# Cross-attention's mask and bias moved into the last row of the keys

## Chip, cores and metric

One core of a Trainium2 chip runs the whole program. The metric is device time in microseconds of that core, the median of several runs. TensorE is called PE below, VectorE DVE, ScalarE ACT, GpSimd POOL; the DMAs are issued by SyncE (SP).

## What is computed

Four blocks in a row: a memory-gated cross-attention (L0), a single-head cross-attention (L1), a six-layer transformer decoder (L2) and a last cross-attention with layer norm (L3). The batch is 8, a sequence has 256 rows of 128 features, the context 64 rows of 64 features. Nearly all of the time goes to the six layers of L2, and the change is in L2's cross-attention:

```python
def _mha(s, t, kv_w, q_w, o_w, o_b, mask):          # 16 heads of 64
    k, v = jnp.split(s @ kv_w, 2, axis=-1)
    q = t @ q_w
    k, v, q = (_heads(k), _heads(v), _heads(q))
    scores = jnp.einsum('bhqd,bhkd->bhqk', q, k) * D ** (-0.5)
    scores = jnp.where(mask[:, None] == 0, jnp.float32(-1000000000.0), scores)
    attn = jax.nn.softmax(scores, axis=-1)
    o = jnp.einsum('bhqk,bhkd->bhqd', attn, v)
    return o.transpose(0, 2, 1, 3).reshape(t.shape[0], t.shape[1], H * D) @ o_w + o_b

def step(t, p):                                      # scanned over 6 layers
    tn = _ln(t, norm_g, norm_b)
    t = _mha(tn, tn, skv, sq, sow, sob, tgt_mask) + t
    tn = _ln(t, norm_g, norm_b)
    t = _mha(src, tn, ckv, cq, cow, cob, src_mask) + t
    tn = _ln(t, pg, pb)
    t = t + (jax.nn.relu(tn @ w1 + b1) @ w2 + b2)
```

`_ln` subtracts the mean, divides by the root of variance plus 1e-5, then multiplies by a gain and adds a bias, one per feature.

## The kernel before

All activations stay in SBUF in f32: `t` holds 16 tiles of 128 rows by 128 features, two per batch entry. The program is not written as a loop. Functions enter steps into a plan with `at(tick, phase, fn)`; at the end the ticks are walked in order, and within a tick the steps in the order of their phase. Each compute engine keeps exactly that order (a manual dependency ties every instruction to the one before it on its engine), so a step with phase 3.7 stands in each engine's queue ahead of one with phase 6 of the same tick, whatever it waits for. DMAs on SP's queue come in program order.

In a layer, self-attention takes 4 ticks per batch entry, 32 in all, then cross-attention takes 2 ticks per entry, 16 in all. `T_ca` is the first tick of the cross-attention. The feed-forward of entry b starts 7 ticks after its cross-attention, and the next layer's self-attention begins inside the cross-attention's last ticks.

PSUM is one pool of four tiles of two banks (lines 35 to 50: `psum`, `two_banks`, with `one_bank`, `tp_tile` and `mm_tile` taking the first half of one). They are handed out in turn, so that a matmul group which asks for a tile waits until the reader of the tile handed out four requests before is done.

The cross-attention of one batch entry (`plan_ca`, with T = T_ca + 2b) works so:

- `ahead` (line 842) makes the normalised input: `moments` on DVE (phase 6 of tick T - 4; `bn_stats` and `bn_aggr`, lines 849 and 850), `scales` on POOL at phase 8.4 (lines 855 to 862: epsilon added, power of -0.5, mean times it, negated), `normal` on ACT (line 868), and `trans` on PE, evicted by ACT with the norm's gain as scale and the norm's bias as bias (lines 882 and 884). Self-attention uses `ahead` too, with `normal` on DVE (line 873), and so does the feed-forward.
- `plan_ca_weights` folds, once per layer, the key and query weights into `AT` and the value and output weights into `WVO` (lines 1083 to 1096). Its first step stands six ticks ahead of T_ca.
- `keys_both` (line 1107) makes the keys of two entries with 16 matmuls (line 1120) into two PSUM tiles, and ACT copies them to SBUF (line 1126). It stands at phase 3.7 of tick T - 2 of every even entry, so at T_ca - 2, + 2, + 6 and + 10.
- `plan_weights_64` (line 329) does one tile of 128 query rows per tick: `scores` (matmuls of line 356, then the mask's matmuls of line 363: bf16, a row of ones against the row of masks `nm2`, accumulated on top), `lower` (ACT copies the scores to SBUF in line 372, DVE takes the maxima per head from PSUM in line 374, POOL subtracts them in line 375), `exps` (ACT, line 381), `divide` (DVE sum and reciprocal, lines 385 and 386, POOL multiplies, line 387), `turn` (DVE transposes, line 395) and `sums` (PE, line 429; DVE adds the residual, line 1145). L0 uses the same function with `mask` None.

Around the change there are also self-attention's `exps` (DVE line 953, ACT line 958), `divide` (DVE line 966, POOL line 968), `turn` (DVE line 978), `values` (PE line 994), `out_proj` (PE line 1012, at phase 3.1) and `add_out` (DVE line 1019, at phase 8.2, which reads `out_proj`'s PSUM tile). The last two of batch entries 6 and 7 fall into the ticks T_ca - 2 and T_ca + 2.

Of the kernel before, what the change touches and what calls it, by code (L numbers as in the profile page):

```python
# [27 lines left out]
def tile_xattn_stack(ctx: ExitStack, tc: tile.TileContext, io, out: bass.AP):  # L28
# [125 lines left out]
    norm_g = column("L2_norm_g")  # L154
    norm_b = column("L2_norm_b")
    pre_g = load_const("L2_pre_gT", [D, NL])
    pre_b = load_const("L2_pre_bT", [D, NL])
# [106 lines left out]

    nm2 = const.tile([P, B, M], BF16, tag="nm2", name="nm2")
    nc.vector.memset(nm2, 0.0)
    ones0 = const.tile([P, 32], BF16, tag="ones0", name="ones0")
    nc.vector.memset(ones0, 0.0)
    nc.vector.memset(ones0[0:1], 1.0)

# [57 lines left out]

    def plan_weights_64(tick, qt, qT, keys, values, mask, take):

# [4 lines left out]
        def scores():  # L335
            sc = two_banks("sc").rearrange("p (q x) -> p q x", q=4)
            if mask is None:
                for i in range(4):
# [14 lines left out]
            for q in range(4):  # L353
                qb = 4 * qt + q
                for a in range(4):
                    nc.tensor.matmul(  # L356
                        sc[32 * a : 32 * a + 32, q, :],
                        lhsT=qT()[:, qb * 32 : (qb + 1) * 32],
                        rhs=keys()[:, a].rearrange("p h k -> p (h k)"),
                        start=True, stop=False,  # L360
                    )
                for a in range(4):
                    nc.tensor.matmul(
                        sc[32 * a : 32 * a + 32, q, :], lhsT=ones0, rhs=mask,
                        start=False, stop=True,
                    )
            tl["sc"] = sc.rearrange("p q x -> p (q x)")

        def lower():
            sc = tl.pop("sc")  # L370
            e = big("e", shape=(P, 16, M))
            nc.scalar.copy(e.rearrange("p h k -> p (h k)"), sc)  # L372
            m = sm([P, 16], "m16")
            nc.vector.tensor_reduce(m, sc.rearrange("p (h k) -> p h k", k=M), AX.X, ALU.max)  # L374
            nc.gpsimd.tensor_tensor(  # L375
                e, e, m.unsqueeze(2).to_broadcast([P, 16, M]), ALU.subtract
            )
            tl["e"] = e
# [12 lines left out]
        def turn():  # L391
            e = tl.pop("e").rearrange("p (q h) (k x) -> p (h k) q x", q=4, x=32)
            eT = big("k" if mask is None else "o", shape=(P, 8, 4, 32))
            for i in range(2):
# [41 lines left out]
        at(tick, 2, lower)  # L436
        if mask is None:
            at(tick + 1, 2.05, exps)
# [197 lines left out]
    def mask_keys():  # L636
        mi = big("q", dtype=I32)
        mi = mi[0:1, : B * M].rearrange("p (b m) -> p b m", b=B)
        nc.sync.dma_start(out=mi, in_=io["mask_Bx1xS2_if1"].rearrange("b o m -> o b m"))
        nc.vector.tensor_scalar(nm2[0:1], mi, 0.0, -BIG, ALU.is_equal, ALU.mult)  # L640

# [41 lines left out]
    def plan_l0(b, T):  # L683
# [88 lines left out]
        for qt in range(QT):  # L772
            plan_weights_64(
                T + qt, qt, lambda: st["q"], lambda: st["k"], lambda: st["VW"], None,
                lambda ps, qt=qt: add(qt, ps),
            )
# [66 lines left out]
    def ahead(b, stats_at, normal_at, tT_at, g, bias, st, on_scalar=True):  # L843

        def moments():
            st["mv"] = sm([P, QT, 2], "mv")
            for j in range(QT):
                six = sm([P, 6], "six")
                nc.vector.bn_stats(six, tt(b)[:, j, :])
                nc.vector.bn_aggr(st["mv"][:, j, :], six)  # L850

        def scales():
            mv = st["mv"]
            ve = sm([P, QT], "ve")
# [191 lines left out]
    def plan_ca_weights(l, T):  # L1046
# [55 lines left out]
        at(T + 1, 8.05, regrouped)  # L1102
        at(T + 2, 3.6, folded("AT", 0, lambda c: st[1][:, :, c, :], HD ** -0.5))
        at(T + 3, 3.6, folded("WVO", 1, lambda c: W["ca", l][2][:, c, :]))

    keys_of = {}

    def plan_ca(l, b, T):
# [3 lines left out]
        def keys_both():  # L1112

            res = [big("q", shape=(D, 4, 4, M)) for _ in range(2)]
            for g in range(2):
# [9 lines left out]
                for i in range(2):  # L1125
                    nc.scalar.copy(
                        res[i][:, :, 2 * g : 2 * g + 2, :].rearrange("p a r k -> p r a k"),
                        ps[:, :, :, i * M : (i + 1) * M],
                    )
            keys_of[b], keys_of[b + 1] = res  # L1130
# [6 lines left out]

        ahead(b, (T - 4, 6), (T - 3, 2.95), (T - 2, 2.9), norm_g, norm_b, st)
        if b % 2 == 0:
# [7 lines left out]
        for qt in range(QT):  # L1147
            plan_weights_64(
                T + qt, qt, lambda: st["tT"], lambda: keys_of[b], lambda: st["VW"],
                nm2[:, b].unsqueeze(1).to_broadcast([P, 4, M]), lambda ps, qt=qt: add(qt, ps),  # L1150
            )
# [229 lines left out]
```

## Time and profile before

| | |
|---|---|
| Time, three runs | median 2428.22 us (2428.0 to 2430.0) |
| The profiled execution's own time | 2429.18 us |
| Its span, first to last instruction | 2427.5 us |
| Mean granted PE clock | 0.984 of full speed |
| PE busy | 2334.8 us (96%) |
| DVE busy | 1833.6 us (76%) |
| ACT busy | 1708.2 us (70%) |
| POOL busy | 1418.0 us (58%) |
| Mask matmuls, line 363 | 1536, 113.6 us busy, 276 ns each, four at a time |
| Score matmuls, line 356 | 3072 records, 221.8 us busy |
| Key copies on ACT, line 1126 | 96, 49.3 us |
| Maxima on DVE, line 374 | 112, 136.7 us |
| Epsilon on POOL, line 855 | 144, 31.7 us |
| Negation on POOL, line 862 | 96, 21.8 us |

An f32 matmul shows as two records. Busy time is the union of an engine's intervals, and a matmul's end is modelled, so a busy PE is not PE at its peak. "Idle before" in a row is the time in which the engine did nothing just ahead of that instruction, with the instruction that ended it behind the arrow. Times of day are microseconds from the start of the span. A layer is about 373 us: line 356 first runs at 395.1 us in the first layer and at 768.0 us in the second. In the second layer, which is used below, T_ca - 2 begins at 754.2 us, T_ca at 768.0, T_ca + 2 at 777.6, T_ca + 3 at 786.9, T_ca + 10 at 833.0.

### The profile page before, as it was taken

The numbers are of one execution on the slowest core, as the hardware profiler recorded it, in microseconds if no ns is written. First come the engines' busy times: TensorE is split into PE (matmuls) and PEld (weight loads), VectorE is DVE, ScalarE is ACT, GpSimd is POOL, SyncE is SP. The second block draws the span as 40 slices with busy tenths as digits, with TensorE's granted clock in tenths as the row PEclk, the third lists the DMA queues.
The fourth block names the chain that finished last, engine by engine and source line by source line (L and its number), as shares of the span: only waits on it lengthen the run. The fifth ranks groups of instructions, "written<-read, shape, count | busy, mean of one in ns | idle before, by whom it ended". The sixth has DMA issues, their size and how long they took to land.

```text
span 2427.5 us, 100277 instructions
## 1 busy us (share of the span) xinstructions
PE 2334.8 (96%) x42564; PEld 1726.5 (71%) x42564; DVE 1833.6 (76%) x5997; ACT 1708.2 (70%) x4514; POOL 1418.0 (58%) x2471
## 2 busy tenths in 40 slices
PE   7889999999999999999999999999999999999997
PEld 4557777677777777777777777777777677777775
DVE  5678887667887767888667888667888667888675
ACT  4567777667777667777667778567778657777653
POOL 2445556755556754556765555765555765455774
PEclk9989999999999999999999999999999999999998
DMA  6000022001022001012000012000013000001000
GB/s 178 2 11 12 20 73 65 2 3 30 21 68 69 2 3 30 20 60 68 12 3 28 22 53 74 12 2 18 25 44 84 21 1 18 25 27 40 2 4 16
DMA packets 102833, 76.88 MB, mean 32 GB/s; under 512 B 8113, under 2 KB 96881, under 8 KB 102386
## 3 DMA queue, kind: packets, MB, share of 16 engines
q1 hardware_dynamic: 101794, 70.16, 9.9%
q8 instruction: 334, 5.47, 0.9%
q14 instruction: 113, 0.93, 0.1%
q10 hardware_dynamic: 592, 0.33, 0.1%
HBM read 62.07 MB, written 8.39 MB: 29 GB/s over the span
## 4 chain that ended last, share of the span: by engine, by line
PE 79%; DVE 8%; ACT 7%; POOL 5%; issue 1%; DMA 0%; ACTq 0%; POOLq 0%; DVEq 0%
PE sc L939 14%; PE mm L902 14%; PE mm L994 14%; PE mm L1012 7%; PE mm L921 7%; PE mm L429 5%; PE sc L356 4%; PE mm L1178 3%; PE mm L1161 3%; DVE m L374 2%; PE mm L1120 2%; PE tp L882 1%; ACT e L958 1%; ACT e L372 1%; PE mm L318 1%
## 5 line engine op out<-in xcount | busy, mean ns | idle before, releaser
L968 POOL TENSOR_SCALAR e<-e,rs 128x256 f32<-128x256 f32 x1536 | 703.0, 478 | 682.4 <-DVE rs L966 673.2
L958 ACT ACTIVATE e<-e,mn 128x256 f32<-128x256 f32 x1536 | 758.2, 495 | 141.6 <-DVE mn L953 137.4
L953 DVE CUSTOM_DVE_ANT_0 e<-sc,nm 128x256 f32<-128x256 f32 x1536 | 542.3, 419 | 102.3 <-PE sc L939 102.1
L978 DVE STREAM_TRANSPOSE eTc<-e 128x512 f32<-128x512 f32 x768 | 517.3, 695 | 62.1 <-POOL e L968 60.9
L939 PE MATMUL sc<-k,q 64*32 64x256 f32 x12288 | 381.0, 383 | 1.1 <-ACT v L301 0.6
L994 PE MATMUL mm<-eTc,v 32*64 32x256 f32 x12288 | 363.6, 378 | 5.7 <-ACT AT L1095 3.3
L375 POOL TENSOR_TENSOR e<-e,m 128x1024 f32<-128x1024 f32 x112 | 213.0, 1902 | 225.3 <-DVE m L374 225.3
L994 PEld LDWEIGHTS mm<-eTc,v 32*64 32x64 f32 x12288 | 277.4, 131 | 88.5 <-issue 22.3
L374 DVE TENSOR_REDUCE m<-sc 128x16 f32<-128x1024 f32 x112 | 136.7, 1220 | 242.7 <-ACT e L372 242.7
L939 PEld LDWEIGHTS sc<-k,q 64*32 64x32 f32 x12288 | 222.0, 107 | 124.0 <-issue 51.4
L958 ACT ACTIVATION_READ_ACCUMULATOR e<-e,mn 128x1 f32 x1536 | 287.1, 187 | 0.0
L356 PE MATMUL sc<-q,tT 128*32 128x256 f32 x3072 | 221.8, 388 | 2.3 <-DVE t L1145 2.3
L429 PE MATMUL mm<-v,o 128*128 128x128 f32 x1536 | 199.8, 285 | 0.2 <-ACT v L324 0.2
L429 PEld LDWEIGHTS mm<-v,o 128*128 128x128 f32 x1536 | 186.3, 198 | 15.9 <-issue 8.1
L902 PE MATMUL mm<-tT,w_sk 128*128 128x256 f32 x768 | 189.3, 389 | 0.0
L1012 PEld LDWEIGHTS mm<-w_sow,o 128*128 128x128 f32 x1536 | 175.1, 192 | 17.6 <-issue 12.3
L921 PE MATMUL mm<-w_sv,tT 128*32 128x256 f32 x3072 | 185.6, 382 | 0.0
L1012 PE MATMUL mm<-w_sow,o 128*128 128x128 f32 x1536 | 183.6, 278 | 1.3 <-ACT WVO L1093 1.3
L301 ACT COPY v<-mm 128x1024 f32<-128x1024 f32 x96 | 97.2, 1012 | 123.2 <-PE mm L921 122.6
L387 POOL TENSOR_TENSOR e<-e,r 128x1024 f32<-128x1024 f32 x96 | 182.6, 1902 | 0.5 <-DVE r L386 0.5
L902 PE MATMUL mm<-tT,w_sq 128*128 128x256 f32 x768 | 173.6, 379 | 0.0
L902 PEld LDWEIGHTS mm<-tT,w_sk 128*128 128x128 f32 x768 | 138.2, 190 | 44.2 <-issue 29.2
(222 smaller groups left out, 3500.8 us busy)
## 6 DMA issues: line engine op xcount, KB each, us to landing
nm<-mask_d SPq DMA_DIRECT2D x192, 128.0 KB
wd<-o SPq DMA_DIRECT2D x48, 128.0 KB
w_sk<-in_L_sa_kv_dram SPq DMA_DIRECT2D x6, 512.0 KB
w_sv<-in_L_sa_kv_dram SPq DMA_DIRECT2D x24, 128.0 KB
w_sq<-in_L_sa_q_dram SPq DMA_DIRECT2D x6, 512.0 KB
w_sow<-in_L_sa_ow_dram SPq DMA_DIRECT2D x6, 512.0 KB
w_ckv<-in_L_ca_kv_dram SPq DMA_DIRECT2D x12, 256.0 KB
w_cq<-in_L_ca_q_dram SPq DMA_DIRECT2D x6, 512.0 KB
```

Of the source, the lines that this page charges most:

```text
L356: nc.tensor.matmul(sc[32 * a : 32 * a + 32, q, :], lhsT=qT()[:, qb * 32 : (qb + 1) * 32], rhs=keys()[:, a].rearrange("p h k -> p (h k)"), ...
L375: nc.gpsimd.tensor_tensor(e, e, m.unsqueeze(2).to_broadcast([P, 16, M]), ALU.subtract)
L429: nc.tensor.matmul(ps[:, :D], lhsT=eT[:, s].rearrange("p q x -> p (q x)"), rhs=vw[:, r, k, g, :], start=(s == 0), stop=(s == 7),)
L902: nc.tensor.matmul(ps[:, i * S : (i + 1) * S], lhsT=w[:, c * P : (c + 1) * P], rhs=st["tT"], start=True, stop=True,)
L921: nc.tensor.matmul(ps[32 * a : 32 * a + 32, i, :], lhsT=st["tT"][:, kb * 32 : (kb + 1) * 32], rhs=sv[:, a].rearrange("p g x -> p (g x)"), ...
L939: nc.tensor.matmul(sc[32 * a : 32 * a + 32, r, j, :], lhsT=st["q"][g][rows, a, qb * 32 : (qb + 1) * 32], rhs=st["k"][g][rows, a, :], start ...
L953: nc.vector.tensor_tensor_reduce(e[:, i, :], sc4[:, i, :], st["nm"][:, 2 * jj + i % 2, :], -1.0, 3.0 * BIG, ALU.add, ALU.min, mn[:, i : i ...
L958: nc.scalar.activation(e[:, i, :], e[:, i, :], AF.Exp, scale=-1.0, bias=mn[:, i : i + 1], accum_out=rs[:, i : i + 1],)
L968: nc.gpsimd.tensor_scalar(e[:, i, :], e[:, i, :], rs[:, i : i + 1], 1.0, ALU.mult, ALU.mult)
L978: nc.vector.transpose(eT[:, r, :, 2 * jj : 2 * jj + 2, :], e[:, 2 * r : 2 * r + 2, :].rearrange("p j (k x) -> p k j x", x=32),)
L994: nc.tensor.matmul(ops[a // 2][r * HD : (r + 1) * HD, a % 2, :S], lhsT=st["v"][kb // 4][rows, kb % 4, (2 * g + r) * HD : (2 * g + r + 1) * ...
L1012: nc.tensor.matmul(st["ps"][:, j * D : (j + 1) * D], lhsT=st["oT"][c // 4][:, c % 4, j * P : (j + 1) * P], rhs=sow[:, c, :], start=(c == 0 ...
```

## The change

The queries' normalised rows sum to zero over the 128 features, so that one feature can be told from the others. The change frees the last one. `trans` in cross-attention now multiplies by `last_off` and adds `last_on`: the gain and bias of the norm are no longer applied there, and the last feature becomes 1. The gain goes into `AT` (`scale`), what the lost feature would have given is subtracted from the other rows of it (`lose_last`), and the bias' contribution becomes the last row (`meet_bias`, `sum_bias`, `put_bias`). The mask is added to that last row as the keys leave PSUM, so that the matmuls of line 363 go. The diff, cut to its core:

```diff
+    norm_rows = const.tile([P, 2, D], F32, tag="norm_rows", name="norm_rows")
+    for i, name in enumerate(("L2_norm_g", "L2_norm_b")):
+        nc.sync.dma_start(out=norm_rows[:, i, :], in_=io[name].partition_broadcast(P))
...
-    nm2 = const.tile([P, B, M], BF16, tag="nm2", name="nm2")
+    nm2 = const.tile([P, B, M], F32, tag="nm2", name="nm2")
+    last_on = ident[:, P - 1 : P]
+    last_off = const.tile([P, 1], F32, tag="last_off", name="last_off")
+    nc.vector.tensor_scalar(last_off, last_on, -1.0, 1.0, ALU.mult, ALU.add)
+    last_big = const.tile([P, 1], F32, tag="last_big", name="last_big")
+    nc.vector.tensor_scalar(last_big, last_on, -BIG, None, ALU.mult)
...
-                        start=True, stop=False,
-                    )
-                for a in range(4):
-                    nc.tensor.matmul(
-                        sc[32 * a : 32 * a + 32, q, :], lhsT=ones0, rhs=mask,
-                        start=False, stop=True,
+                        start=True, stop=True,
...
-            nc.vector.tensor_reduce(m, sc.rearrange("p (h k) -> p h k", k=M), AX.X, ALU.max)
+            nc.vector.tensor_reduce(m, e, AX.X, ALU.max)
...
-        nc.sync.dma_start(out=mi, in_=io["mask_Bx1xS2_if1"].rearrange("b o m -> o b m"))
-        nc.vector.tensor_scalar(nm2[0:1], mi, 0.0, -BIG, ALU.is_equal, ALU.mult)
+        nc.sync.dma_start(
+            out=mi, in_=io["mask_Bx1xS2_if1"].rearrange("b o m -> (b o) m").partition_broadcast(P)
+        )
+        nc.vector.tensor_scalar(nm2, mi, 0.0, last_big, ALU.is_equal, ALU.mult)
...
+            st["ve"] = sm([P, QT], "ve")
+            nc.vector.tensor_scalar(st["ve"], st["mv"][:, :, 1], 1e-5, None, ALU.add)
+            if on_scalar:
+                st["mneg"] = sm([P, QT], "mneg")
+                nc.vector.tensor_scalar(st["mneg"], st["mv"][:, :, 0], -1.0, None, ALU.mult)
 
         def scales():
-            mv = st["mv"]
-            ve = sm([P, QT], "ve")
-            nc.gpsimd.tensor_scalar(ve, mv[:, :, 1], 1e-5, None, ALU.add)
             st["rstd"] = sm([P, QT], "rstd")
-            nc.gpsimd.tensor_tensor(st["rstd"], ve, mhalf, ALU.pow)
+            nc.gpsimd.tensor_tensor(st["rstd"], st["ve"], mhalf, ALU.pow)
             if on_scalar:
-                nm = sm([P, QT], "nm")
-                nc.gpsimd.tensor_tensor(nm, mv[:, :, 0], st["rstd"], ALU.mult)
                 st["nm"] = sm([P, QT], "nm2")
-                nc.gpsimd.tensor_scalar(st["nm"], nm, -1.0, None, ALU.mult)
+                nc.gpsimd.tensor_tensor(st["nm"], st["mneg"], st["rstd"], ALU.mult)
...
+        def meet_bias():
+            st["z"] = big("q", shape=(P, HC, D))
+            nc.gpsimd.tensor_tensor(st["z"], st["AT"], rows(1), ALU.mult)
+        def sum_bias():
+            st["add"] = sm([P, HC], "add")
+            nc.vector.tensor_reduce(st["add"], st.pop("z"), AX.X, ALU.add)
+        def scale():
+            nc.gpsimd.tensor_tensor(st["AT"], st["AT"], rows(0), ALU.mult)
+        def lose_last():
+            last = sm([P, HC], "last")
+            nc.gpsimd.tensor_copy(last, st["AT"][:, :, D - 1])
+            nc.gpsimd.tensor_tensor(
+                st["AT"], st["AT"], last.unsqueeze(2).to_broadcast([P, HC, D]), ALU.subtract
+            )
+        def put_bias():
+            nc.gpsimd.tensor_copy(st["AT"][:, :, D - 1], st.pop("add"))
+        at(T + 2, 8.05, meet_bias)
+        at(T + 3, 2.35, scale)
+        at(T + 3, 8.05, lose_last)
+        at(T + 3, 8.7, sum_bias)
+        at(T + 4, -0.1, put_bias)
...
-                    nc.scalar.copy(
+                    nc.vector.tensor_tensor(
                         res[i][:, :, 2 * g : 2 * g + 2, :].rearrange("p a r k -> p r a k"),
                         ps[:, :, :, i * M : (i + 1) * M],
+                        nm2[:, b + i].unsqueeze(1).unsqueeze(1).to_broadcast([P, 2, 4, M]),
+                        ALU.add,
                     )
...
-        ahead(b, (T - 4, 6), (T - 3, 2.95), (T - 2, 2.9), norm_g, norm_b, st)
+        ahead(b, (T - 4, 6), (T - 3, 2.95), (T - 2, 2.9), last_off, last_on, st)
...
-        plan_ca_weights(l, T_ca - 6)
+        plan_ca_weights(l, T_ca - 7)
```

So per layer: 256 matmuls go from PE, 16 copies leave ACT and become 16 additions on DVE at the same place of the plan (phase 3.7), 24 epsilon additions and 16 negations go from POOL to DVE's `moments` (phase 6, or 8.3 for self-attention), three POOL passes over `AT`, two small POOL copies and one DVE sum are new, and the folding starts one tick earlier.

More of the change, by code (lines that the diff above doesn't have):

```diff
@@ L262, in load_mask @@
         return nm
-    nm2 = const.tile([P, B, M], BF16, tag="nm2", name="nm2")
[L266 to L269, printed above, removed]
+    nm2 = const.tile([P, B, M], F32, tag="nm2", name="nm2")
[4 more added lines that the diff above has]
+    nc.vector.tensor_scalar(last_big, last_on, -BIG, None, ALU.mult)
     def stats(xin, eps):
@@ L327, in values_of, with plan_weights_64 @@
         return vw
-    def plan_weights_64(tick, qt, qT, keys, values, mask, take):
+    def plan_weights_64(tick, qt, qT, keys, values, halves, take):
         tl = {}
@@ L336, in scores @@
             sc = two_banks("sc").rearrange("p (q x) -> p q x", q=4)
-            if mask is None:
+            if halves:
                 for i in range(4):
@@ L392, in turn @@
             e = tl.pop("e").rearrange("p (q h) (k x) -> p (h k) q x", q=4, x=32)
-            eT = big("k" if mask is None else "o", shape=(P, 8, 4, 32))
+            eT = big("k" if halves else "o", shape=(P, 8, 4, 32))
             for i in range(2):
@@ L436, in plan_weights_64 @@
         at(tick, 2, lower)
-        if mask is None:
+        if halves:
             at(tick + 1, 2.05, exps)
@@ L637, in mask_keys @@
         mi = big("q", dtype=I32)
-        mi = mi[0:1, : B * M].rearrange("p (b m) -> p b m", b=B)
-        nc.sync.dma_start(out=mi, in_=io["mask_Bx1xS2_if1"].rearrange("b o m -> o b m"))
-        nc.vector.tensor_scalar(nm2[0:1], mi, 0.0, -BIG, ALU.is_equal, ALU.mult)
+        mi = mi[:, : B * M].rearrange("p (b m) -> p b m", b=B)
+        nc.sync.dma_start(
+            out=mi, in_=io["mask_Bx1xS2_if1"].rearrange("b o m -> (b o) m").partition_broadcast(P)
+        )
+        nc.vector.tensor_scalar(nm2, mi, 0.0, last_big, ALU.is_equal, ALU.mult)
     mask_bf = []
@@ L773, in plan_l0 @@
             plan_weights_64(
-                T + qt, qt, lambda: st["q"], lambda: st["k"], lambda: st["VW"], None,
+                T + qt, qt, lambda: st["q"], lambda: st["k"], lambda: st["VW"], True,
                 lambda ps, qt=qt: add(qt, ps),
@@ L1103, in plan_ca_weights, with rows @@
         at(T + 2, 3.6, folded("AT", 0, lambda c: st[1][:, :, c, :], HD ** -0.5))
+        def rows(i):
+            return norm_rows[:, i].unsqueeze(1).to_broadcast([P, HC, D])
+        def meet_bias():
[19 more added lines that the diff above has]
+        at(T + 4, -0.1, put_bias)
         at(T + 3, 3.6, folded("WVO", 1, lambda c: W["ca", l][2][:, c, :]))
@@ L1149, in plan_ca @@
                 T + qt, qt, lambda: st["tT"], lambda: keys_of[b], lambda: st["VW"],
-                nm2[:, b].unsqueeze(1).to_broadcast([P, 4, M]), lambda ps, qt=qt: add(qt, ps),
+                False, lambda ps, qt=qt: add(qt, ps),
             )
```

## The prediction

> **What bounds the kernel now.** I read the page's busy shares and chain, then the busy time by stage, then the waits, the chain and the timeline of one cross-attention.
>
> ```profile
> PE 2334.8 (96%) x42564; PEld 1726.5 (71%) x42564; DVE 1833.6 (76%) x5997; ACT 1708.2 (70%) x4514; POOL 1418.0 (58%) x2471
> PE 79%; DVE 8%; ACT 7%; POOL 5%; issue 1%; DMA 0%; ACTq 0%; POOLq 0%; DVEq 0%
> ...
> 490.00:770.00 280.00, 278.48 (x5550) 208.24 (x5552) 223.76 (x821) 214.86 (x635) 153.89 (x314) 1.00 0.13 39
> 777.00:855.00 78.00, 72.63 (x1066) 55.43 (x1048) 52.91 (x108) 49.23 (x81) 60.52 (x69) 0.98 0.04 9
> ```
>
> Columns of the last two: stretch, length, busy PE, PE's loads, DVE, ACT, POOL, clock. In self-attention PE works 278.48 of 280 us. In cross-attention it works 72.63 of 78, and POOL 60.52. The stage is bound twice: by PE, and by a loop over ACT, DVE and POOL which is about as long.
>
> **What goes: the mask's matmuls.** The chain shows what they cost:
>
> ```profile
> 787.54 0.11 PE sc L363 x4
> 787.65 0.43 PE sc L356 x8
> ```
>
> Four run at once, so a group costs 0.11 us, not its 0.28 us duration. A query tile has four groups, a layer 16 tiles: 0.44 x 16 = 7.0 us per layer, 42 us in all, wherever PE sets the pace.
>
> **What moves to DVE: the key copies.** Each is 128x512 out of PSUM with a second operand in SBUF. The only row of that shape is line 458, 691 ns; the 128x1024 one of line 631 takes 1206 ns, so each further 512 elements costs 0.52. I take 0.65 for one of a run (bounds 0.52 and 0.69): 2.6 us per key build, against 2.05 on ACT. The sum matters less than the place. Tick T_ca - 2:
>
> ```profile
> 759.50 0.13 DVE L966 RECIPROCAL rs<-rs 128x4 f32<-128x4 f32 x1
> 760.51 2.06 PE L1120 MATMUL mm<-ctx,AT 64*128 64x128 f32 x32
> 760.88 1.42 DVE L978 STREAM_TRANSPOSE eTc<-e 128x512 f32<-128x512 f32 x2
> 761.72 2.05 ACT L1126 COPY q<-mm 128x512 f32<-128x512 f32 x4 [0.37 <-PE mm L1120]
> 762.23 0.39 DVE L1019 TENSOR_TENSOR t<-mm,tb 128x256 f32<-128x256 f32 x1
> 762.49 1.48 PEld L939 LDWEIGHTS sc<-k,q 64*32 64x32 f32 x64
> ```
>
> At phase 3.7 the additions stand behind the reciprocal that ends at 759.63 and ahead of `moments`, the second reciprocal, the transposes and `add_out`, line 1019. Today DVE does all that while PE is still at line 1012 and line 1120. Afterwards it must stand until the first half of the keys is there (761.72, where ACT starts now): additions to 764.3, `moments` 0.87 (759.55 to 760.42) and two new small operations at 0.13 each (a reciprocal of 128x4 takes 0.13) to 765.45, reciprocal 0.15, transposes 1.42, `add_out` 0.39: it ends at 767.4, not 762.62. Who waits for it is told by the four PSUM tiles. In order, PE asks here for out-projection, keys, keys, scores, scores; the second scores get the out-projection's tile. The waits agree with this count: in self-attention, where the order is out-projection, values' projection, scores, scores, `values`, it is `values` that waits for line 1019.
>
> ```profile
> PEld mm L994 <- DVE t L1019: 2.5, 6, 0.4
> ```
>
> Those scores could start at 762.49 + 0.98 = 763.47. PE stands 3.9 us (2.9 if additions cost 0.52 and transposes overlap; 4.1 at 0.69).
>
> Tick T_ca + 2 has the same trap, one tile nearer (out-projection, values, keys, keys, scores):
>
> ```profile
> 784.50 1.24 DVE L395 STREAM_TRANSPOSE o<-e 128x512 f32<-128x512 f32 x2
> 784.87 2.06 PE L1120 MATMUL mm<-ctx,AT 64*128 64x128 f32 x32
> 786.44 0.40 DVE L1019 TENSOR_TENSOR t<-mm,tb 128x256 f32<-128x256 f32 x1
> 786.90 0.16 PEld L356 LDWEIGHTS sc<-q,tT 128*32 128x32 f32 x8 [0.17 <-DVE t L1019]
> ...
> PEld sc L356 <- DVE t L1019: 1.0, 6, 0.2
> ```
>
> The last line is from the waits of the whole run: six times, once a layer, PE waits there already now. With the additions from 785.74 to 788.35, `moments` with its two new operations to about 789.45 and `add_out` to 789.85, PE, which would be ready 0.44 earlier at 786.5, stands 3.4 us (2.9 to 3.6). At T_ca + 6 and T_ca + 10 the scores take the tile of line 1145, which DVE empties ahead of the additions. At T_ca + 6 the additions delay the maxima by 0.4 (812.5 plus 2.6, plus 1.63 of `moments` and 0.5 of new operations, against 816.79), and ACT there waits for line 1161 anyway: nothing. At T_ca + 10 three `moments` follow and the maxima (845.26) come 2.1 late; what is late next is line 873, then PE's transposes behind it: 1.3 (0 to 2.1).
>
> **What moves from POOL to DVE: epsilon and negation.** POOL saves 0.30 + 0.29 per normalisation with their gaps (801.43 to 801.73, 802.80 to 803.11), so 1.2 us where two follow each other, at T_ca + 4 and T_ca + 8 ahead of line 375. DVE's price has a row against it:
>
> ```profile
> 847.94 1.90 POOL L375 TENSOR_TENSOR e<-e,m 128x1024 f32<-128x1024 f32 x1
> 848.98 2.81 DVE L873 TENSOR_SCALAR xn<-t,mv,rstd 128x128 f32<-128x128 f32 x2
> 849.80 1.90 POOL L387 TENSOR_TENSOR e<-e,r 128x1024 f32<-128x1024 f32 x1
> ```
>
> Two DVE operations of 0.31 us each (the line's minimum) take 2.81: each ends as a POOL instruction ends. The new operations are the same kind, SBUF to SBUF with scalars. At T_ca + 4 the first waits for line 387 (to 800.66), its neighbour for line 305 (to 801.35), the second pair up to another 0.8: the next maxima begin at 802.5 to 803.3, not 801.09, and end by 804.5, when POOL would be free at 803.5. Of 1.2 us some 0.1 to 0.9 remains. Since the loop there, not PE, opens the gap of 2.70 us ahead of line 882 at 806.05, the seven ticks T_ca + 3 to + 9 follow the masks' 3.1 us only in part. I take 1.5 of it, so 1.6 is not harvested (0 to 2.6).
>
> The Trainium skill, "SBUF — State Buffer", section "SBUF: two separate sides", calls this an exclusive lock: whichever of a two-port DVE operation and a POOL operation starts first has the shared ports for its whole instruction. By that rule any of the 240 new DVE operations can wait out a whole POOL pass, 1.90 at most, or make POOL wait; the sum would move to the third rival.
>
> **The clock.** After the gap of 2.70 the stretch 806 to 813 ran at 0.76:
>
> ```profile
> 806.00:813.00 7.00, 6.89 (x80) 5.96 (x82) 4.35 (x9) 4.71 (x7) 5.54 (x4) 0.76 0.01 2
> ```
>
> That is 1.7 us lost of 7. Two new gaps of over 3 us can bring two more (3.4), the old one may go (-1.7). I take +1.0.
>
> "TensorE: Matmul & The Clock Gate", section "What's actually happening", has the clock halved after an idle window of about 3.4 us; by it the gap of 2.70 would be too short, which the row denies, and only the new gaps would pay, an estimate of 2 x 1.7 per layer.
>
> **Priced at nothing.** The maxima from SBUF: line 374 already waits for ACT's copy of the same scores (242.7 us over 87 waits), and a sum of the same shape from SBUF, line 385, takes 1208 ns against 1220. The PSUM tile comes free 1.2 earlier, but nobody waits for line 374 beyond 0.7 us in all. POOL's passes over `AT`, 3 x 1.9 (as line 375) and two copies, fall into the self-attention's end, where POOL idles 2.3 to 2.8 us ahead of each group of line 968; without that cover the transposes of line 978 come up to 1.5 late per layer. DVE's sum of `z`, 1.2, lies there too, and the keys read `AT` more than a tick later. Folding one tick earlier only reorders PE. ACT's 2.05 per key build is relief that no wait asks for. At the start two more DMAs of 64 KB stand on SP ahead of weights needed late, and the mask's DMA grows to all partitions with one DVE operation waiting behind it: 0 to 3 us once.
>
> **The sum**, per layer: -7.0 masks, +3.9 at T_ca - 2, +3.4 at T_ca + 2, +1.3 at T_ca + 10, +1.6 not harvested, +1.0 clock = +4.2, so 25 us over six layers. The profiled execution took 2429.18 with a span of 2427.5; the runs' median is 2428.2, a microsecond less, and I add to that: **2453 us**. With every low bound it is -7.0 + 2.9 + 2.9 + 0 + 0 - 1.7 = -2.9 per layer (2411), with every high one -7.0 + 4.1 + 3.6 + 2.1 + 2.6 + 3.4 + 1.5 = +10.3 (2490); not all at once, so the case's own range is 2434 to 2474.
>
> **Rivals.**
> - *Faster (0.27).* The additions do not hold PE. It decides at `add_out`: if line 1019 still ends before line 1120 does, the two stands (7.3) and their clock (1.0) go, and 4.2 becomes -4.1 per layer: 2404. For it: 242.7 us of DVE's waits at line 374 show room on that engine. Against it: the room lies behind line 1019, not ahead of it.
> - *No change (0.10).* Half of the stands are caught by slack, for instance because ACT, free of the copies, runs ahead: 4.2 - 4.2, 2428. For it: PE already idles 5.4 of the 78 us above, which new idle time may replace. Against: both stands come where PE has no gap today.
> - *Much slower (0.13).* DVE becomes the stage's bound. Per four ticks it has 19.6 us now (four times 3.9, two `moments` of 1.6, two of 0.4); 2.6, eight small operations and up to 5 us of waits for POOL make 28, the period of today. A microsecond more per entry is 8 x 6 = 48 minus what is counted above: about 2485. Against: POOL gets emptier as it waits.
>
> **How the numbers follow.** The forecast has 0.50. A measurement tells 0.2%, 4.9 us, from no change. Slower takes the forecast and the third rival, 0.63; same 0.10; faster 0.27. The range runs from 2404, the faster rival's middle, to 2480: about 0.13 lies below, under 0.07 above.
>
> **What would show it.** Line 363 is gone and PE's busy time falls by far more than the span. In the waits, PE at line 939 (or its loads) waits for line 1019 once a layer for about 4 us, and at line 356 once for about 3. Line 1107's additions show as DVE operations of 0.5 to 0.7 us, idle ahead of the first one at T_ca - 2 some 2 us for line 1120. The small DVE operations have a median near 0.13 and a tail to 1.9. I am wrong if line 1019 ends on time, or if the scores take another PSUM tile.

## The result, and the profile after

The changed kernel takes 2432.24 us (median of 20 runs, 2428.52 to 2436.07) against 2428.15 us for the kernel before (20 runs, 2426.36 to 2433.38). The ratio is 1.0016 with a 95% interval of 1.001 to 1.0022, so the change costs about 4 us where 25 were forecast. The profiled execution took 2432.26 us, with a span of 2430.5. Line numbers are those of the kernel after unless another kernel is named: 356 became 362 (scores), 1019 became 1022 (`add_out`), 1120 became 1153 and 1126 became 1159 (keys), 994 became 997 (`values`), 374 and 375 became 375 and 376, 873 became 876, 882 became 885.

Page of the kernel after, the busy shares and the shares of the chain:

```profile
PE 2308.7 (95%) x41028; PEld 1691.6 (70%) x41028; DVE 1930.7 (79%) x6338; ACT 1658.9 (68%) x4418; POOL 1401.4 (58%) x2261
...
PE 73%; DVE 15%; POOL 6%; ACT 4%; issue 2%; DMA 0%; POOLq 0%; ACTq 0%; DVEq 0%
```

PE lost 1536 matmuls and 26 us of busy time, and the span grew all the same. The end is set less by PE (73% of the chain, was 79%) and nearly twice as much by DVE (15%, was 8%), which took on 97 us.

Busy time by stretch in the kernel after (columns as before: stretch, length, busy PE, its loads, DVE, ACT, POOL, clock). The first line is self-attention, the second a cross-attention of the same layer, the last two lie in its end:

```profile
490.00:770.00 280.00, 275.08 (x5355) 205.34 (x5361) 226.18 (x831) 208.55 (x613) 155.06 (x294) 1.00 0.13 37
780.00:858.00 78.00, 71.26 (x960) 52.61 (x942) 62.11 (x139) 44.64 (x71) 56.82 (x52) 0.96 0.03 9
850.40:853.80 3.40, 0.18 (x1) 0.14 (x1) 3.37 (x6) 1.12 (x3) 3.40 (x3) 1.00 0.00 0
853.90:857.30 3.40, 3.10 (x30) 1.49 (x33) 0.79 (x3) 1.51 (x2) 0.17 (x1) 0.50 0.02 5
```

In the 78 us DVE works 62.11 where it worked 52.91, POOL 56.82 where it worked 60.52, and PE is idle 6.7, more than the 5.4 of before, though it has less to do. The last pair is the reading to remember: for 3.40 us PE has almost nothing, DVE and POOL are full, and then PE has its work at half the clock.

**T_ca - 2**, timeline of the kernel after (start, duration, instruction, idle time before it and what ended that):

```profile
763.33 2.06 PE L1153 MATMUL mm<-ctx,AT 64*128 64x128 f32 x32
...
764.61 2.45 DVE L1159 TENSOR_TENSOR q<-mm,nm 128x512 f32<-128x512 f32 x4
...
765.64 1.96 PE L942 MATMUL sc<-k,q 64*32 64x256 f32 x64 [0.26 <-ACT tT L887]
...
767.53 0.66 PE L997 MATMUL mm<-eTc,v 32*64 32x256 f32 x8
...
769.33 0.38 DVE L1022 TENSOR_TENSOR t<-mm,tb 128x256 f32<-128x256 f32 x1
...
769.77 3.06 PE L997 MATMUL mm<-eTc,v 32*64 32x256 f32 x104 [1.58 <-DVE t L1022]
```

The additions take 2.45 us (0.65 each was forecast, 2.6), and `add_out` ends at 769.71. As everything lies 2.8 us later than before here, that is 766.9 on the old time, where the prediction had 767.4. DVE's side of the step was right. But the scores of line 942 run at 765.64 without waiting for it. It is the second tile of `values` that stands, for 1.58 us and not 3.9.

**T_ca + 2**, timeline of the kernel after:

```profile
789.69 2.06 PE L1153 MATMUL mm<-ctx,AT 64*128 64x128 f32 x32
...
790.90 2.48 DVE L1159 TENSOR_TENSOR q<-mm,nm 128x512 f32<-128x512 f32 x4 [0.22 <-PE mm L1153]
...
791.67 1.93 PE L362 MATMUL sc<-q,tT 128*32 128x256 f32 x32
...
794.37 0.42 DVE L1022 TENSOR_TENSOR t<-mm,tb 128x256 f32<-128x256 f32 x1
```

The scores start right behind the keys, 3.1 us before `add_out` ends. They were given another PSUM tile; the stand of 3.4 us isn't there at all. In the kernel before, the scores at this place do wait for `add_out` (the prediction shows the row).

**T_ca + 10**, timeline of the kernel after:

```profile
842.80 2.46 DVE L1159 TENSOR_TENSOR q<-mm,nm 128x512 f32<-128x512 f32 x4
...
848.34 1.21 DVE L375 TENSOR_REDUCE m<-e 128x16 f32<-128x1024 f32 x1
848.41 1.95 PE L1213 MATMUL mm<-w_f,o 128*128 128x128 f32 x16
...
852.05 2.11 DVE L876 TENSOR_SCALAR xn<-t,mv,rstd 128x128 f32<-128x128 f32 x2
...
853.62 0.30 PE L885 MATMUL tp<-ident,xn 128*128 128x128 f32 x1 [3.26 <-DVE xn L876]
```

Between the additions and the maxima DVE does three `moments` (845.19 to 848.43). The maxima start at 848.34, against 845.26 before; 0.7 of the 3.1 us is the lag that PE has there already (line 1196 runs at 846.68, its counterpart in before at 846.0), so they are 2.4 late (2.1 was forecast). All that follows on DVE is late by it, line 876 at the end, and PE idles 3.26 us for it, which is the empty stretch shown above.

Waits of the whole run, kernel after:

```profile
PE tp L885 <- DVE xn L876: 17.7, 10, 3.3
PEld mm L997 <- DVE t L1022: 12.5, 6, 2.3
PE mm L997 <- DVE t L1022: 9.8, 6, 1.9
```

The first was 9.4 us before. The other two are one wait, seen by PE's loads and by its matmuls, six times in the run, once a layer.

### The profile page after: what moved, and what is told of

It reads as the page before. It is cut to its first block, busy times and chain, and to the rows that moved or that the text cites. A ratio compares the mean times of both kernels' runs of the same rounds, so it can differ in the third digit from the quotient of the medians.

```text
span 2430.5 us, 97314 instructions
## 1 busy us (share of the span) xinstructions
PE 2308.7 (95%) x41028; PEld 1691.6 (70%) x41028; DVE 1930.7 (79%) x6338; ACT 1658.9 (68%) x4418; POOL 1401.4 (58%) x2261
## 4 chain that ended last, share of the span: by engine, by line
PE 73%; DVE 15%; POOL 6%; ACT 4%; issue 2%; DMA 0%; POOLq 0%; ACTq 0%; DVEq 0%
PE mm L905 14%; PE sc L942 13%; PE mm L997 13%; PE mm L924 7%; PE mm L1015 7%; PE mm L430 4%; PE mm L1213 3%; PE sc L362 3%; PE mm L1196 2%; DVE m L375 2%; DVE q L1159 2%; DVE e L956 2%; POOL e L971 2%; DVE eTc L981 2%; PE tp L885 1%
## 5 line engine op out<-in xcount | busy, mean ns | idle before, releaser
L997 PE MATMUL mm<-eTc,v 32*64 32x256 f32 x12288 | 368.7, 379 | 24.7 <-DVE t L1022 9.8
L375 DVE TENSOR_REDUCE m<-e 128x16 f32<-128x1024 f32 x112 | 136.3, 1217 | 150.2 <-ACT e L373 150.2
L362 PE MATMUL sc<-q,tT 128*32 128x256 f32 x3072 | 192.6, 393 | 3.1 <-DVE t L1180 3.1
```

The costliest lines, as they stand in the source:

```text
L362: nc.tensor.matmul(sc[32 * a : 32 * a + 32, q, :], lhsT=qT()[:, qb * 32 : (qb + 1) * 32], rhs=keys()[:, a].rearrange("p h k -> p (h k)"), ...
L997: nc.tensor.matmul(ops[a // 2][r * HD : (r + 1) * HD, a % 2, :S], lhsT=st["v"][kb // 4][rows, kb % 4, (2 * g + r) * HD : (2 * g + r + 1) * ...
```

## The experiments

Each ratio is against runs of the kernel before on the same chip.

| Run | us | ratio to before | 95% interval |
|---|---|---|---|
| kernel after | 2432.24 | 1.0016 | 1.001 to 1.0022 |
| before_no_masks | 2414.57 | 0.994 | 0.9928 to 0.9953 |
| before_dve_norm | 2407.69 | 0.9907 | 0.9893 to 0.9921 |
| no_masks_dve_norm | 2391.14 | 0.9841 | 0.9827 to 0.9854 |
| before_dve_keys | 2458.16 | 1.012 | 1.0106 to 1.0134 |
| after_pool_norm | 2467.25 | 1.015 | 1.0136 to 1.0164 |
| after_psum_max | 2433.93 | 1.0015 | 1.0006 to 1.0024 |
| after_act_keys | 2410.10 | 0.9927 | 0.9914 to 0.9941 |
| after_no_passes | 2426.17 | 0.9992 | 0.9983 to 1.0 |
| act_keys_no_passes | 2390.42 | 0.9847 | 0.9833 to 0.986 |
| after_fold_9 | 2445.03 | 1.0058 | 1.0046 to 1.0071 |
| after_addout_first | 2429.28 | 0.9996 | 0.9987 to 1.0005 |
| after_row_mask | 2439.22 | 1.0035 | 1.0023 to 1.0047 |
| row_mask_late_pass | 2440.82 | 1.0045 | 1.0033 to 1.0058 |
| after_last_keys_act | 2411.23 | 0.993 | 0.9917 to 0.9942 |
| after_first_keys_act | 2426.89 | 0.9992 | 0.9984 to 1.0001 |

**What the masks are worth alone** (before_no_masks).

```diff
-                        start=True, stop=False,
+                        start=True, stop=True,
                     )
-                for a in range(4):
-                    nc.tensor.matmul(
-                        sc[32 * a : 32 * a + 32, q, :], lhsT=ones0, rhs=mask,
-                        start=False, stop=True,
-                    )
```

> The kernel before with nothing changed except that the mask's matmuls (line 363) are left out of the cross-attention, so the mask is not applied. Theory A (removing the masks is worth most of 7.0 us per layer, and other parts of the change eat it up): about 2390 us, 2384 to 2404, which is 4 to 7.4 us per layer below the kernel before. Theory B (the loop over ACT, DVE and POOL binds the cross-attention as tightly as PE does, so the masks were never worth much): 2416 to 2428, at most 2 us per layer.

2414.57, 13.1 us less than before (2427.7 in this comparison), 2.2 us of the 7.0 per layer. That falls to theory B, just beyond its bound. Waits of this run (its line 877 is line 882 of before, where the same row has 20.6 us in 13 waits):

```profile
PE tp L877 <- ACT xn L863: 33.4, 24, 3.2
```

PE reaches its transposes earlier and stands there for the normalised rows. In the profiled executions PE's busy time falls by 37.9 us (2334.8 to 2296.9) and the span by 19.9; this wait takes 12.8 of the 18 us between them. Where the rest went was not separated.

**The key copies on DVE alone** (before_dve_keys).

```diff
-                    nc.scalar.copy(
+                    nc.vector.tensor_copy(
```

> The kernel before with its key copies moved from ACT to DVE and nothing else. The prediction's step (additions ahead of add_out hold PE 3.9 us at T_ca-2 and 3.4 us at T_ca+2, and 1.3 at T_ca+10): +40 to +55 us, so 2468 to 2483. Theory A as the trace of after suggests it (one stand of about 2 us per layer, at `values`, and some lateness at the end of the stage): 2438 to 2452. Theory B: 2424 to 2434, since PE catches up in the stage anyway.

+30.5 us, which no theory had: 6 us above what the trace of after suggested and 10 us short of the prediction's. The scores at T_ca + 2 no longer wait for `add_out`, as they do in the kernel before. The wait of `values` for `add_out` is there too, 9.5 us in six waits. The transposes' wait for ACT's normalised rows rises as well, from 20.6 to 33.0 us.

**ACT's key copies in the kernel after** (after_act_keys), the same part undone: the addition of line 1159 becomes `nc.scalar.copy` of the same slices.

> The kernel after with its key additions replaced by ACT's copies, as in the kernel before; the mask is left out. Theory A: the stand of `values` behind add_out goes and with it 2 to 2.5 us per layer and a part of the lateness at the end of the stage: 2412 to 2422. Theory B: 2429 to 2435, no change against after.

2410.10: 17.6 us below before (2427.7), where after is 4.1 above, so 21.7 below after. Theory A, a little more than it said. So the key additions on DVE cost about 22 us, not 52 (8.6 x 6). Waits of this run, of which the kernel after has neither:

```profile
PE sc L942 <- DVE t L1022: 4.9, 5, 1.0
PE sc L362 <- DVE t L1022: 4.1, 6, 0.7
```

With ACT emptying the keys' tiles, the scores of both places wait for `add_out`, those of line 942 at their second tile, just as the prediction counted; with DVE emptying them, `values` does.

**POOL's passes over AT** (after_no_passes). The five `at(...)` lines of `meet_bias`, `scale`, `lose_last`, `sum_bias` and `put_bias` are taken out.

> The kernel after with the five steps on AT left out (two multiplications, the subtraction of the last column, the sum and the copy of it on POOL and DVE), so the keys are made from AT as it was folded. Theory A, second half (POOL's passes in the tail of self-attention make rstd, the normalised rows and PE's transposes late): 2.0 to 2.4 us per layer come back, 2417 to 2421, and the wait of PE's transposes at the first cross-attention entry (1.13 us at 758.57 in the trace of after) goes. What the prediction said (hidden, priced at nothing, at most 1.5 per layer): 2423 to 2433.

2426.17: about 6 us below after (1.0016 - 0.9992 = 0.0024), not the 11 to 15 of theory A and within what the prediction allowed. The trace says more than the time: the wait of the transposes at the first entry is gone. What it was, in the timeline of after:

```profile
750.75 2.36 POOL L1120 TENSOR_TENSOR AT<-AT,norm_rows 128x1024 f32<-128x1024 f32 x1
...
755.16 1.90 POOL L1125 TENSOR_TENSOR AT<-AT,last 128x1024 f32<-128x1024 f32 x1
...
757.01 0.70 POOL L862 TENSOR_TENSOR rstd<-ve,mhalf 128x2 f32<-128x2 f32 x1
...
757.79 0.20 POOL L865 TENSOR_TENSOR nm<-mneg,rstd 128x2 f32<-128x2 f32 x1
...
758.02 0.88 ACT L871 ACTIVATE xn<-t,nm,rstd 128x128 f32<-128x128 f32 x2 [0.90 <-POOL nm L865]
...
758.57 0.71 PE L885 MATMUL tp<-ident,xn 128*128 128x128 f32 x2 [1.13 <-ACT xn L871]
```

POOL starts `rstd` the moment the pass ends, ACT waits for it, PE waits for ACT. POOL was idle here before, and that idle time was no cover, since a small, urgent step lies in the same place. But PE, arriving earlier, now stands longer at the next wait: `values` for `add_out` rises from 9.8 to 11.3 us. The passes' price is hidden behind the additions' price; the run act_keys_no_passes below takes both away.

**add_out ahead of the additions** (after_addout_first).

```diff
-        at(T + 6, 8.2, add_out)
+        at(T + 6, 3.65, add_out)
```

> The kernel after with add_out planned at phase 3.65 instead of 8.2, so that DVE empties the out-projection's tile before the key additions and not behind them; nothing is left out. If the place of the additions in DVE's order holds PE (the prediction's step at T_ca-2, seen in the trace of after as `values` waiting for add_out, 1.6 to 2.3 us a layer): that wait goes and 9 to 16 us come back, 2416 to 2423. If it is DVE's time as such, which makes everything behind it late: 2428 to 2434. What is lost at T_ca+12 (2.7 us a layer) should stay in both.

2429.28, about 5 us less than after (1.0016 - 0.9996 = 0.002), which lies in the range of "DVE's time as such". The wait of `values` for `add_out` is gone, all 9.8 us of it, and the transposes' wait for ACT's normalised rows rises from 20.2 to 30.9. The stand is real, but taking it away wins only 5 us, since PE waits longer at the next place.

**Epsilon and negation back on POOL** (after_pool_norm).

```diff
-            st["ve"] = sm([P, QT], "ve")
-            nc.vector.tensor_scalar(st["ve"], st["mv"][:, :, 1], 1e-5, None, ALU.add)
...
+            nc.gpsimd.tensor_scalar(ve, mv[:, :, 1], 1e-5, None, ALU.add)
```

(and the negation in the same way)

> The kernel after with epsilon and the negated mean back on POOL; nothing is left out. Without the masks alone PE's transposes waited 33.4 us for ACT's normalised rows and only 13 us were won; in the run with ACT's key copies, which has epsilon and negation on DVE, they waited 19.1 and 22 us more were won than in after. If the moved epsilon and negation are what lets the masks' time be taken: 2442 to 2452, and that wait rises above 30 us. By the prediction (of 1.2 us that POOL saves, 0.1 to 0.9 remains at two of eight entries): 2433 to 2438.

2467.25, +33 us against after (1.015 - 1.0016 = 0.0134 of 2428 us). That is far beyond both ranges: the edit which the prediction priced at almost nothing is the largest of all. Waits of this run, where the kernel after has 20.2 us in 18 waits:

```profile
PE tp L885 <- ACT xn L871: 50.5, 29, 3.2
```

The wait grows by 30.3 us. That this is near the whole difference is chance: the transposes' wait for DVE (line 876) falls at the same time from 17.7 to 6.6 us. Of the 34.5 us by which the profiled span grows, 17.7 are PE's busy time (2308.7 to 2326.4, for the same matmuls), as the mean granted clock falls from 0.980 to 0.971.

**Maxima from PSUM** (after_psum_max): line 375 reads `sc` again.

> The kernel after with the maxima read from the scores in PSUM, as before; nothing is left out. By the prediction (maxima wait for ACT's copy of the same scores anyway, priced at nothing): 2429 to 2436. If the earlier release of the scores' tile is where a part of the masks' time is won: 2438 or more.

2433.93, ratio 1.0015 against 1.0016: nothing, as predicted.

**The fold two ticks earlier** (after_fold_9): `plan_ca_weights(l, T_ca - 7)` becomes `T_ca - 9`.

> The kernel after with the weights of cross-attention folded from T_ca-9 on instead of T_ca-7, which takes POOL's passes and the WVO copy out of self-attention's last two ticks into its steady part; nothing is left out. If the passes cost by their place: as without them, 2423 to 2428, since the wait for add_out at the first entry takes half of it back. If they cost by POOL's time alone wherever they are, or the fold disturbs its new place: 2430 to 2436.

2445.03, about 10 us more than after and above both ranges. In the whole run `values` now waits for the transposes of the weights 12 times (12.0 us), where it does so 6 times (5.2 us) in after. POOL's mean share of 55% in self-attention's steady part (155 of 280 us) said nothing of that. But the fold's own matmuls and copies move too, so what the passes alone cost there isn't shown.

**Normalisation on DVE in the kernel before, with masks and without** (before_dve_norm, no_masks_dve_norm). The first is the edit of after_pool_norm reversed, made to the kernel before; the second takes the masks away as well.

> The kernel before with epsilon and the negated mean on DVE and nothing else. If the chain from moments over POOL's rstd to ACT's normalised rows is what binds the stage beside PE (theory C: the masks' time can be taken only as this chain gets shorter): 2414 to 2422, with fewer waits of PE's transposes for the normalised rows than the 20.6 us of before. If PE binds while the masks are there: 2425 to 2429.

> The kernel before with the mask's matmuls left out and epsilon and the negated mean on DVE; the mask is not applied. Theory C: the two together win more than the sum of each alone, 2396 to 2406, about what is left when POOL's passes (6 us) are taken from the run with ACT's key copies (2410.1). If each has its own price: before_dve_norm's gain added to the 13 us of the masks alone.

2407.69, 21.9 us below before, and 2391.14, 38.4 below (before is 2429.54 here). Both are faster than their ranges. The sum of each alone is 13.1 + 21.9 = 35.0, so the two are nearly additive; of theory C's claim that the masks' time can only be taken with this edit, no more than the 3.4 us between 35.0 and 38.4 remains, which is about the width of the intervals. Waits of before_dve_norm, whose row was 20.6 us in 13 waits in before, and its timeline at T_ca + 10:

```profile
PE tp L882 <- ACT xn L868: 9.7, 8, 2.1
```

```profile
840.14 1.23 DVE L374 TENSOR_REDUCE m<-sc 128x16 f32<-128x1024 f32 x1 [0.43 <-ACT e L372]
841.45 1.90 POOL L375 TENSOR_TENSOR e<-e,m 128x1024 f32<-128x1024 f32 x1 [0.74 <-DVE m L374]
...
843.87 2.11 DVE L873 TENSOR_SCALAR xn<-t,mv,rstd 128x128 f32<-128x128 f32 x2
```

POOL's pass follows the maxima at once. In before the maxima ended at 846.49 and the pass began at 847.94 (the row is in the prediction): POOL was still busy with three normalisations in a row, ten small instructions. This kernel computes the whole reference, and it is the fastest here that does: it beats both the kernel before and the kernel after.

**The mask on the copied keys** (after_row_mask), and one pass moved in it (row_mask_late_pass).

```diff
+        def mask_last():
+            for i in range(2):
+                row = keys_of[b + i][96:].rearrange("p a r k -> p (a r) k")
+                nc.vector.tensor_tensor(
+                    row, row, nm2[96:, b + i].unsqueeze(1).to_broadcast([32, 16, M]), ALU.add
+                )
...
             at(T - 2, 3.7, keys_both)
+            at(T - 2, 8.25, mask_last)
```

The second run has `at(T + 3, 8.5, lose_last)` in place of 8.05.

> The kernel after with the keys copied by ACT as before, and the mask added afterwards by DVE to the last 32 partitions of the copied keys (32x1024, two per key build), planned at phase 8.25, behind add_out; nothing is left out. DVE has about the same time to spend as in after, but nothing of it stands between PE and add_out or moments. If it is the place of the additions that costs: 2410 to 2417. If it is DVE's time: 2425 to 2434.

> The run after_row_mask with one line moved: the subtraction of AT's last column on POOL goes from phase 8.05 to 8.5 of its tick, behind the rstd of the first cross-attention entry instead of ahead of it; nothing is left out. If it is this pass that makes the first transposes late (1.13 us at 758.57 in the trace of after): 5 to 10 us less than after_row_mask. If the passes cost wherever they lie: the same within 3 us.

2439.22 and 2440.82. The first is slower than after, beyond the range of "it is DVE's time"; the place alone is refuted. Two additions on 32 partitions take 2.36 us together, as long as four on 128 from PSUM. At T_ca + 10 they are still ahead of the maxima and of line 876 (timeline of after_row_mask):

```profile
848.44 2.36 DVE L1168 TENSOR_TENSOR q<-q,nm 32x1024 f32<-32x1024 f32 x2
...
851.83 1.21 DVE L375 TENSOR_REDUCE m<-e 128x16 f32<-128x1024 f32 x1
...
857.11 0.45 PE L885 MATMUL tp<-ident,xn 128*128 128x128 f32 x1 [3.49 <-DVE xn L876]
```

The second run differs from the first by less than their intervals: moving this pass behind `rstd` doesn't help, so that one order is not what the passes cost by. That it is POOL's time wherever they lie fits, but isn't shown.

**Which key build pays** (after_last_keys_act, after_first_keys_act). A condition ahead of the addition sends one build of a layer's four to ACT.

```diff
+                    if b == B - 2:
+                        nc.scalar.copy(
...
+                        continue
```

The other run has `b == 0`.

> The kernel after with ACT's copy for the last of a layer's four key builds (T_ca+10), whose two entries lose their mask; the other three builds stay additions on DVE. If the additions cost most where three `moments` and the next layer's normalised rows follow them on DVE (the trace of after loses 2.7 us a layer at T_ca+12, after_row_mask 3.7): 2414 to 2420, and PE's waits for line 876 fall from 17.7 to about 6 us. If the four builds share the 22 us evenly: 2426 to 2428.

> The kernel after with ACT's copy for the first of a layer's four key builds (T_ca-2), whose two entries lose their mask; the other three stay additions on DVE. The prediction's 3.9 us a layer at T_ca-2, seen as 1.6 to 2.3 at `values` in the trace of after: with nothing taken back later, 2418 to 2423; if what this wait frees is lost in the next one, as when add_out went first (5 us): 2425 to 2429.

2411.23 and 2426.89: 21 us (1.0016 - 0.993 = 0.0086) and 6 us (0.0024) below after. The last build, T_ca + 10, is worth as much as all four together, somewhat more than expected; the first is worth what after_addout_first won. Timeline of after_last_keys_act at T_ca + 10:

```profile
837.67 2.05 ACT L1160 COPY q<-mm 128x512 f32<-128x512 f32 x4
...
842.12 1.21 DVE L375 TENSOR_REDUCE m<-e 128x16 f32<-128x1024 f32 x1
...
845.83 2.11 DVE L876 TENSOR_SCALAR xn<-t,mv,rstd 128x128 f32<-128x128 f32 x2
...
847.40 0.30 PE L885 MATMUL tp<-ident,xn 128*128 128x128 f32 x1 [0.99 <-DVE xn L876]
```

The gap ahead of line 885 is 0.99 us and not 3.26, and the run's waits for line 876 fall from 17.7 to 6.4 us.

**The passes without the additions** (act_keys_no_passes): after_act_keys and after_no_passes in one.

> The kernel after with ACT's key copies (mask left out) and without the five steps on AT; left of the change are the removed masks, epsilon and negation on DVE, maxima from SBUF and the fold a tick earlier. The run without masks and with normalisation on DVE took 2391.1, the one with ACT's key copies 2410.1; between them stand the passes, the earlier fold and the maxima. If the passes are the whole of it: 2389 to 2396. If the earlier fold has a part of its own: 2398 to 2406.

2390.42. The passes are the whole of it: 20 us between this run and after_act_keys (0.9927 - 0.9847 = 0.008), and nothing beyond the uncertainty left for the earlier fold and the maxima beside no_masks_dve_norm (0.9841).

## Why the prediction was wrong

The sign was right, the size six times too large, and the sign was luck: without POOL's passes, which were priced at nothing, the kernel after is level with before (after_no_passes, 0.9992). The runs make a path from the kernel before to the kernel after, one part at a time, so that the steps add up by construction; each is a difference of two runs, against the runs of before beside them, uncertain by some 3 to 5 us:

| Part, in us over six layers | forecast | measured | between |
|---|---|---|---|
| masks gone, epsilon and negation on DVE | -32 (-7.0 and +1.6 a layer) | -38.4 | before, no_masks_dve_norm |
| earlier fold, maxima from SBUF | 0 | +0.8 | no_masks_dve_norm, act_keys_no_passes |
| passes over AT | 0 | +20.0 | act_keys_no_passes, after_act_keys |
| key additions on DVE, clock with them | +58 (3.9, 3.4, 1.3, 1.0) | +21.7 | after_act_keys, after |
| sum | +25 | +4.1 | |

Another order of the steps would divide the time otherwise: the key copies on DVE cost 30.5 us in the kernel before, and the passes 6 when the additions stay.

**The step that failed first: "the second scores get the out-projection's tile".** It rested on PSUM tiles handed out in turn, counted from the order of the requests in before. In the kernel after they weren't: neither the scores at T_ca - 2 nor those at T_ca + 2 take that tile. The count was right for keys emptied by ACT (before, after_act_keys); that it would hold when DVE empties them was the mistake. Moving the copies alone moves the tile (before_dve_keys), with the requests in the same order, so the pool doesn't simply go round, as the section on the kernel before has it. How it chooses stays open. The 3.4 us at T_ca + 2 are 0, and the 3.9 at T_ca - 2 are a stand of 1.58 at `values`, worth 6 us in the whole run by after_first_keys_act, 1 a layer. The prediction had named this itself ("if the scores take another PSUM tile"). Together the two stands were 44 of its 52 us of additions.

**T_ca + 10 was under-priced.** The mechanism was right to 0.3 us (maxima 2.4 late, line 876 late, the transposes behind it), but 1.3 us a layer was put down for it. The last build costs 21 us, 3.5 a layer. The gap of 3.26 us also costs half the clock of the next 3.41 us, in five layers of after and in none of after_last_keys_act. That makes an estimate: 5 x 1.7 = 8.5 us of clock and 11.3 us less waiting (17.7 to 6.4) are 19.8 of the 21. The prediction laid its clock term, +1.0 a layer, at the two stands that weren't there. In the two profiles half clock lasts 37.5 us in after and 34.1 in before (stretches that begin between 300 and 2400 us), which is 1.7 us more lost, not 6.

**"Of 1.2 us some 0.1 to 0.9 remains" failed.** The edit is worth 21.9 us in the kernel before and 33 in the kernel after. Two things were wrong. The saving was looked for at T_ca + 4 and T_ca + 8 only, while at T_ca + 10 three normalisations follow each other on POOL ahead of the pass. And at T_ca + 4 itself the small DVE operations were expected to wait for POOL for most of the time saved. Timeline of before, then of before_dve_norm, at T_ca + 4:

```profile
798.76 1.90 POOL L387 TENSOR_TENSOR e<-e,r 128x1024 f32<-128x1024 f32 x1
801.09 1.19 DVE L374 TENSOR_REDUCE m<-sc 128x16 f32<-128x1024 f32 x1
804.66 1.90 POOL L375 TENSOR_TENSOR e<-e,m 128x1024 f32<-128x1024 f32 x1
```

```profile
797.02 1.90 POOL L387 TENSOR_TENSOR e<-e,r 128x1024 f32<-128x1024 f32 x1
800.00 1.22 DVE L374 TENSOR_REDUCE m<-sc 128x16 f32<-128x1024 f32 x1
801.41 1.90 POOL L375 TENSOR_TENSOR e<-e,m 128x1024 f32<-128x1024 f32 x1
```

Counted from line 387, the maxima come 0.65 us later (1.4 to 2.2 were forecast), and the next pass begins 1.5 us earlier (0.1 to 0.9). The waits exist, but they are short. In the kernel after:

```profile
L858 DVE TENSOR_SCALAR mneg<-mv x96: 154/160/771, 376.8 to 2396.7; 128x2 f32<-128x2 f32 x96
```

The minimum is 154 ns, the median 160, the longest 771. There 50 of the 240 new operations (lines 855 and 858) take more than 0.2 us, and each of these ends 0.02 to 0.03 us after a POOL instruction does. One of the longest stands beside a whole instruction of POOL (timeline of the kernel after):

```profile
527.53 0.77 DVE L858 TENSOR_SCALAR mneg<-mv 128x2 f32<-128x2 f32 x1
527.55 0.72 POOL L311 TENSOR_TENSOR tb<-t,w_cob 128x256 f32<-128x256 f32 x1
```

That agrees with the Trainium skill's rule of the exclusive lock ("SBUF — State Buffer", section "SBUF: two separate sides"), on which the third rival leaned, as line 873's 2.81 us in before does. But none of the 240 began more than 0.26 us before the end of a pass of 1.90, so none waited one out; and 27 of them ended while POOL was still at an `rstd` (line 862), 5 while it was at line 971, where the rule doesn't show. All this waiting together is about 10 us of DVE in the whole run. The edit's worth also has a part from the clock: PE's busy time falls from 2334.8 us in before to 2325.0 in before_dve_norm, for the same matmuls.

**The masks' 7.0 us a layer were right as PE's work and wrong as time.** Alone they bring 2.2. The prediction's net of 5.4 came out near the measured 6.4 because normalisation brought what the masks did not: two errors of opposite sign in one line, which is luck.

**"POOL's passes fall into the self-attention's end, where POOL idles" failed**: nothing was forecast, at most 1.5 a layer, and 3.3 was measured. They take 2.36, 2.37 and 1.90 us rather than three times 1.9, and `rstd` and self-attention's weights queue behind them. In the kernel after only 6 of these 20 us show when the passes alone go, because the additions then catch PE at the next wait. How the other 14 divide between that wait, the stage's later waits and the clock was not separated.

What was right: 0.65 us an addition (2.45 measured for four in a row, 0.61 each), the DVE order ahead of `add_out`, no price for the maxima and the earlier fold.

## What to carry to other kernels

Before pricing a wait for a buffer, find in the trace which instruction waits for that release today, and don't take it for granted afterwards: here the tile's next user changed because another engine emptied its neighbours. A small run with that one edit (before_dve_keys) would have told. An engine's idle time is cover only if nothing urgent is queued behind the work put there; look at the small steps (here `rstd`, 0.70 us) and not at the idle sum. In a loop that is bound by several engines, the cheapest instructions on its chain can be worth more than the most numerous ones beside it: a change made of several parts should be tried part by part, as here one part (normalisation on VectorE) is a gain of 0.9% that the others hide.

## What the runs showed of the hardware

**The half clock comes in windows on a fixed grid.** In each of the 17 traces the stretches of half clock start on one grid of 3.41 us and last a multiple of it, but for one at the program's end. I compared PE's idle time in each window of the grid (between 300 and 2370 us, not itself at half clock) with the clock of the next one: of 90 windows with 1.9 us of idle time or more, all 90 were followed by half clock; of 142 with 1.3 to 1.9 us, 70; of the 9879 with less, none. It need not be one gap: in row_mask_late_pass two of 0.92 and 0.99 us in one window (at 766.6) were enough. The Trainium skill, "TensorE: Matmul & The Clock Gate", section "What's actually happening", speaks of an idle window of about 3.4 us; the length agrees, but about half of it idle is enough here. Two stretches of the kernel after, each with the one that follows it:

```profile
806.10:809.50 3.40, 1.63 (x23) 0.76 (x16) 3.37 (x7) 1.72 (x5) 3.24 (x6) 1.00 0.00 0
809.55:812.95 3.40, 3.27 (x16) 2.88 (x15) 2.03 (x4) 2.75 (x4) 1.94 (x2) 0.50 0.02 7
1178.20:1181.60 3.40, 1.69 (x33) 0.79 (x21) 3.29 (x8) 1.45 (x4) 3.24 (x6) 1.00 0.00 0
1181.65:1185.05 3.40, 3.07 (x36) 2.50 (x43) 2.03 (x4) 3.02 (x5) 2.18 (x2) 1.00 0.00 0
```

The same place in two layers, with 1.63 and 1.69 us of work for PE: half clock follows the first and not the second. So a gap near 1.7 us costs 1.7 more or nothing, and parts of a change don't add up exactly. What decides between 1.3 and 1.9 us isn't shown; idle time alone doesn't, since in the same trace a window with 1.47 us of it (from 1874.5, in gaps of 1.13, 0.28 and 0.06) was followed by half clock.

**Partitions don't shorten an addition.** On DVE 32x1024 took 1234 ns (48 instructions in after_row_mask), about what the one of 128x1024 in before took (1206, line 631, which reads PSUM). On POOL the second operand's pattern counts: for 128x1024, a row of 128 values repeated eight times costs 2.36 us (line 1120), and one value repeated 128 times, for each of eight blocks, 1.90 (line 1125).
